# Down stage: two operands read a step earlier, weights a product later

## The chip, the cores and the metric

The kernel runs on one core of a Trainium2 chip. The metric is the device time of one execution in microseconds; the lower the better. One launch computes the whole block, and all arithmetic is done on the core. The core has five engines that run side by side, each with its own instruction order: PE multiplies matrices, ACT applies functions and scaled copies, DVE and POOL work elementwise, and SP issues the DMAs in this program.

## The reference

The block has an attention part and a feed-forward part, each with a residual and a layer norm. The change lies in the last product of the feed-forward part.

```python
x = _layernorm(x + _L0_attn_ref(x, Wq, Wk, Wv, Wo))
x = _layernorm(x + _L0_ffn_ref(x, ...))

def _L0_ffn_ref(input, SU_ug, SU_dp, Wscale_ug, Wscale_dp, W_up, W_gate, W_down):
    x = fwht(x * SU_ug) / SCALE                  # 4096 tokens x 512
    x_up = x @ W_up.T * (Wscale_ug[:INTER] * SCALE)
    x_gate = x @ W_gate.T * (Wscale_ug[INTER:] * SCALE)
    x = jax.nn.silu(x_gate) * x_up               # 4096 x 2048
    x = fwht(x * SU_dp) / SCALE
    x = x @ W_down.T * (Wscale_dp * SCALE)       # 4096 x 512
```

`fwht` is a Walsh-Hadamard transform. The kernel moves the second one into the weights: it transforms W_down once, so that the down product works on silu(gate) times up directly.

## The kernel before

**Arithmetic.** Every fp32 operand is split into a high and a low half[...]: ACT copies the value with rounding into `hi` (line 95), then DVE or POOL subtracts it from the original into `lo` (line 96). `hilo` does both. Each product then takes three matmuls: high by high, high by low, low by high.

**Gate and up.** The loop over `n` (32 steps) computes blocks of gate and up by a scheme of seven half-size products in place of eight. Step n = 31 is the last. Its results and the sums S1 to S4 of them (made by POOL at line 1117, in `hS`) are the seven left-hand operands of the down stage, and are stored to DRAM in `hop_d` by the closures in `late_puts`. Results and sums live in 16 buffers (`utile`, pool `g1`).

**Down.** The tokens are cut into eight units (`units`), and each unit has seven products, s = 0 to 6; (n, s) is product s of unit n. `order` lists them: first units 0 and 1 in turn, (0,0), (1,0), (0,1), (1,1) and so on, then the other units. A product is 48 matmuls of 128x256 at line 1196, into the PSUM tiles `ps_da`, `ps_dc` and `ps_db`. Its left operand is read from `hop_d` in four pieces of 128x512 (`hraw`, 256 KB each; `h_load`) and split by `h_split` into `hah` and `hal`. For s = 0 the operands of units 0 and 1 have tiles of their own, `hxh` and `hxl`. The weights of product s are read from `wdop_d[s]` in four pieces as well (`braw`; `load_b`), split by `split_b` into `wdh`, `wdl`, `wdzh` and `wdzl`, and stay for all units. In this text the first weights are those of s = 0, the second those of s = 1, and so on. Their reads and splits lie between the products of units 0 and 1. DVE adds each finished product to the residual `yres` (line 1206).

**Memory.** All pieces read in this stage, `hraw` as well as `braw` (and before them the weights of gate and up), share one pool of ten buffers:

```python
    rp = ctx.enter_context(tc.tile_pool(name="rp", bufs=10, reuse_waits="tile"))
```

A read is issued when the piece that had its buffer has been split. The split operands `hah` and `hal` have 19 buffers in the pool `d1`, which lies where the pool `g1` of gate and up lay; such a tile can be written when the result or sum that had its place is out of use, and for a sum that is when its store has landed.

**Order.** The kernel's text sets what depends on what and a priority. A scheduler with a time model of its own then puts each engine's instructions into one fixed order. An engine works its list strictly in that order: if an instruction waits, all behind it on that engine wait as well. That holds for SP's queue of DMAs, too.

Of the kernel before, what the change touches and what calls it, by code (L numbers as in the profile page):

```python
# [43 lines left out]
def kernel(  # L44
# [6 lines left out]
    V, S, G, T = nc.vector, nc.scalar, nc.gpsimd, nc.tensor  # L51
# [895 lines left out]
    def h_load(n, s):  # L947
        f, jp = units[n]
        HR[n, s] = []
        for qd in range(4):  # L950
            raw = rp.tile([128, 2, 256], F32, tag="ar", name="hraw")
            dma(raw, hop_d[f][s, jp, :, 2 * qd:2 * qd + 2])
            HR[n, s].append(raw)

    def load_b(s):
        RAW["b", s] = []
        for j in range(4):
            x = rp.tile([128, 2, 256], F32, tag="ar", name="braw")
            dma(x, wdop_d[s][:, 2 * j:2 * j + 2])
            RAW["b", s].append(x)  # L960
# [33 lines left out]
    with ExitStack() as es:  # L994
        pa = es.enter_context(tc.tile_pool(name="g1", bufs=1, reuse_waits="tile"))

        def utile(name):
            return pa.tile([128, 512], F32, tag="u", name=name, bufs=16)

        def araw(name):  # L1000
            return rp.tile([128, 2, 2, 128], F32, tag="ar", name=name)

        def ff_front(i):
            y2 = []
            for e in range(2):
                y = praw.tile([128, 512], F32, tag="raw", name="y_nat")
                dma(y, y_d[2 * i + e])
                y2.append(y)
            yield
            yield from front(i, y2, pa, lambda s, n: pgu.tile(s, F32, tag="a", name=n, bufs=4),  # L1010
                             lambda s, n: pgu.tile(s, F32, tag="a", name=n, bufs=4), (ytile, xtile))

        for s in range(7):
            aload(1, s, araw("A"))
        NS = 32
        yraw, late_puts = [], []
        fr = None
        for n in range(NS):
            f, p = divmod(n, 8)
            bank, sv, c = {}, {}, {}  # L1020

            def emit(u, q, x):
                if u == 1:
                    S.activation(x, x, AF.Silu)  # L1024
                    c["g", q] = x
                else:
                    G.tensor_tensor(x, x, c.pop(("g", q)), ALU.mult)  # L1027
                    c["h", q] = x

            if n in (1, 3, 5, 8):  # L1030
                step(fr, 12)
                fr = ff_front(12 + (1, 3, 5, 8).index(n))
            new = {}
            for s, tag in enumerate(SEQ):
                first = SEQ.index(tag) == s
                wh, wl = AOP.pop((n, s))
                yh, yl = YOPS[s]
                for u in (1, 0):
                    if first:
                        bank[tag, u] = pgu.tile([128, 512], F32, tag=tag, name="ps_" + tag, bufs=4 if tag == "a" else 2)  # L1040
                    ps = bank[tag, u]
                    i = 0
                    for k in range(2):
                        for w, y in ((wh, yh), (wh, yl), (wl, yh)):
                            T.matmul(ps, w[:, u, k], y[:, k], start=first and i == 0, stop=i == 5,  # L1045
                                     skip_group_check=not first)
                            i += 1
                    it = 2 * p + (s >= 4 and s < 6)
                    sc = wsc[:, u, it:it + 1]
                    if s in (0, 2, 4):  # L1050
                        x = pa.tile([128, 512], F32, tag="sv", name="sv", bufs=6)
                        S.activation(x, ps, AF.Copy, scale=sc)  # L1052
                        sv[s, u] = x
                    if s in (1, 4, 6):
                        src, k, q = {1: (ps, 0, 0), 4: (bank.get(("b", u)), 4, 3), 6: (ps, 2, 1)}[s]
                        x = utile("cc")
                        V.scalar_tensor_tensor(x, src, sc, sv[k, u], ALU.mult, ALU.add)
                        emit(u, q, x)
                    if s == 5:
                        if u == 1:  # L1060
                            x = utile("sg")
                            S.activation(x, ps, AF.Silu, scale=sc)
                            c["g", 2] = x
                        else:
                            x = c.pop(("g", 2))
                            V.scalar_tensor_tensor(x, ps, sc, x, ALU.mult, ALU.mult)  # L1066
                            c["h", 2] = x
                if n and s in (1, 2, 3):
                    for _ in range(3):
                        if late_puts:  # L1070
                            late_puts.pop(0)()
                if n + 1 < NS:
                    asplit(n + 1, s)
                if n + 2 < NS:
                    aload(n + 2, s, araw("A"))
                if p == 7:
                    if f < 3:
                        new[s] = ysplit(s, yraw[s])
                        if s < 5:
                            yraw.append(yload(f + 1, s + 2))  # L1080
                    elif s == 0:
                        hx = [praw.tile([128, 2, 256], F32R, tag="raw", name="hxh") for _ in range(3)]
                        hx.append(wres.tile([128, 2, 256], F32R, tag="w", name="hxh"))
                        hy = [ytile([128, 4, 256], F32R, x) for x in ("hxl", "hxl", "hxh", "hxh", "hxl", "hxl")]
                        h_split_x(0, hx, halves(hy[0:2]))
                        h_load(1, 0)
                        y_load(0, 0)
                        y_load(1, 0)
                    elif s == 2:
                        split_b(0)  # L1090
                        load_b(1)
                    elif s == 3:
                        h_split_x(1, halves(hy[2:4]), halves(hy[4:6]))
                        load_b(2)
                    elif s == 4:
                        split_b(1)
                        h_load(0, 1)
                elif n == NS - 2:
                    if s == 4:
                        h_load(0, 0)  # L1100
                    elif s == 6:
                        load_b(0)
                step(fr)
            if p == 6 and f < 3:
                yraw = [yload(f + 1, 0), yload(f + 1, 1)]
            YOPS.update(new)
            H = {"A11": c["h", 0], "A12": c["h", 2], "A21": c["h", 1], "A22": c["h", 3]}

            def put(key, f=f, p=p, H=H):
                dma(hop_d[f][WKEY.index(key)].rearrange("j p i t -> p j i t")[:, :, p],  # L1110
                    H[key].rearrange("p (j t) -> p j t", j=2))

            late_puts = [lambda k=k, put=put: put(k) for k in ("A11", "A12", "A22", "S1", "S3", "S2", "S4")]
            for key, x0, x1, op in (("S1", "A21", "A22", ALU.add), ("S3", "A11", "A21", ALU.subtract),
                                    ("S2", "S3", "A22", ALU.subtract), ("S4", "A12", "S2", ALU.add)):
                H[key] = utile("h" + key)
                G.tensor_tensor(H[key], H[x0], H[x1], op)  # L1117

    with ExitStack() as es:
        pd = es.enter_context(tc.tile_pool(name="d1", bufs=2, reuse_waits="tile"))  # L1120
        order = [(n, s) for s in range(7) for n in range(2)]
# [4 lines left out]
        def h_split(n, s):  # L1126
            HOP[n, s] = []
            for qd, raw in enumerate(HR.pop((n, s))):
                hi, lo = (pd.tile([128, 2, 256], F32R, tag="ad", name=x, bufs=19) for x in ("hah", "hal"))
                hilo(hi, lo, raw, G if qd == 1 or (qd == 3 and s % 2) else V)  # L1130
                HOP[n, s].append((hi, lo))

        def finish(n, half):
# [22 lines left out]

        todo = None
        for idx, (n, s) in enumerate(order):
            if 0 < idx and idx + 1 < len(order):
                h_split(*order[idx + 1])  # L1160
            if n == 0 and s + 2 < 7:
                split_b(s + 2)
            if 0 < idx and idx + 2 < len(order):
                h_load(*order[idx + 2])
            if n == 1 and s + 3 < 7:
                load_b(s + 3)
            for put in late_puts[:3]:
                put()
            late_puts = late_puts[3:]
            if s == 1 and n < 2:  # L1170
                y_load(n, 1, pd)
            if s == 6 and n == 1:
# [18 lines left out]
            for ip, j in ([(ip, j) for j in range(2) for ip in range(8)] if last else  # L1191
                          [(ip, j) for ip in range(8) for j in range(2)]):
                qd, r = divmod(ip, 2)
# [89 lines left out]
```

## Time and profile before

| what | value |
|---|---|
| median of three runs | 2299.53 us (2297.73 to 2301.41) |
| profiled execution | 2299.27 us |
| its span | 2297.6 us, granted clock 0.994 |
| PE busy | 2258.7 us, 98% of the span |
| DVE, ACT, POOL busy | 1757.2, 1393.8, 1280.1 us |
| first matmul of the down stage | 1950.4 us |
| last matmul of gate and up | 1965.1 us |

The profile tells one execution on one core. Its own time is 1.67 us longer than its span, which runs from the first to the last instruction. Durations and places below are microseconds from the span's start. A busy share is an average over the whole kernel; what a change in one stage is worth is read from the waits in that stage. The granted clock is the share of full speed that TensorE was given: 1.00 or, after some pauses, 0.50.

### The profile page before, as it was taken

Reading aid. Unit: us, or ns where it says so; the run is one execution under the profiler, and the core shown is the slowest. Engines: PE = TensorE matmul, PEld = TensorE weight load, DVE = VectorE, ACT = ScalarE, POOL = GpSimd, SP = SyncE. Lnnn points to the kernel's source line nnn. Section 1 sums busy time; section 2 is a strip of 40 time slices with the busy share of each in tenths; the row PEclk is TensorE's granted clock in tenths of the full one; section 3 lists DMA queues with packets and bytes.
Section 4 is the critical chain, followed back from the end, with each engine's and each line's share of the span. In section 5 each row is a group of like instructions: output and inputs, shape, how many; then the busy total and the mean of one; then the engine's idle time right before and its main releaser. Section 6 shows DMA issues by size and latency. Waiting matters only on the chain. (4 is left out here: it accounts for less than half of the span.)

```text
span 2297.6 us, 42221 instructions
## 1 busy us (share of the span) xinstructions
PE 2258.7 (98%) x14432; PEld 2004.3 (87%) x14432; DVE 1757.2 (76%) x2684; ACT 1393.8 (61%) x2515; POOL 1280.1 (56%) x1063
## 2 busy tenths in 40 slices
PE   8999999999999999899999999999999999999998
PEld 7999999899999998688878878878788888899998
DVE  8888888888888878688898775766766766675555
ACT  7777777777777767444443466665555655464553
POOL 5556666555555545568797535665555555633332
PEclk9999999999999999999999999999999999999999
DMA  6665665555555544889998976876765757887773
GB/s 195 176 181 167 184 181 171 168 156 150 167 165 154 170 135 142 301 271 277 284 285 258 309 252 214 253 239 190 230 208 186 242 185 211 260 276 238 227 251 121
DMA packets 369527, 484.15 MB, mean 211 GB/s; under 512 B 68670, under 2 KB 224384, under 8 KB 365344
## 3 DMA queue, kind: packets, MB, share of 16 engines
q1 hardware_dynamic: 369312, 481.45, 68.4%
q8 instruction: 114, 1.87, 0.3%
q14 instruction: 101, 0.83, 0.1%
HBM read 282.76 MB, written 156.76 MB: 191 GB/s over the span
## 5 line engine op out<-in xcount | busy, mean ns | idle before, releaser
L288 PE MATMUL ps_qk<-xh,wh 128*128 128x256 f32 x1280 | 355.3, 278 | 0.0
L288 PE MATMUL ps_qk<-xl,wh 128*128 128x256 f32 x1280 | 354.9, 277 | 0.0
L288 PE MATMUL ps_qk<-xh,wl 128*128 128x256 f32 x1280 | 354.4, 277 | 0.0
L394 POOL TENSOR_SCALAR_AFFINE_SELECT A<-A 64x512 fp32r<-64x512 f32 x256 | 211.5, 826 | 241.8 <-DVE am L390 145.0
L1027 POOL TENSOR_TENSOR cc<-cc 128x512 f32<-128x512 f32 x96 | 149.0, 1554 | 288.8 <-ACT cc L1024 109.7
L96 DVE TENSOR_TENSOR wol<-A,woh 128x512 fp32r<-128x512 f32 x217 | 223.3, 1036 | 104.4 <-ACT woh L95 92.7
L270 POOL TENSOR_TENSOR sw<-sw,csb 128x512 f32<-128x512 f32 x160 | 208.5, 1303 | 135.2 <-ACT sw L269 124.2
L288 PEld LDWEIGHTS ps_qk<-xh,wh 128*128 128x128 f32 x1280 | 240.7, 188 | 3.0
L288 PEld LDWEIGHTS ps_qk<-xh,wl 128*128 128x128 f32 x1280 | 240.4, 188 | 0.9
L288 PEld LDWEIGHTS ps_qk<-xl,wh 128*128 128x128 f32 x1280 | 240.6, 188 | 0.3
L95 ACT ACTIVATE woh<-A 128x512 fp32r<-128x512 f32 x217 | 135.5, 630 | 134.6 <-PE ps_b L1045 76.5
L95 ACT ACTIVATE hah<-hraw 128x512 fp32r<-128x512 f32 x216 | 133.7, 629 | 125.5 <-PE ps_da L1196 63.8
L96 POOL TENSOR_TENSOR hal<-hraw,hah 128x512 fp32r<-128x512 f32 x78 | 106.9, 1374 | 175.2 <-PE ps_da L1196 75.0
L1045 PE MATMUL ps_a<-yoh,woh 128*128 128x512 f32 x512 | 202.6, 397 | 1.2 <-ACT sv L1052 1.0
L1045 PE MATMUL ps_a<-yol,woh 128*128 128x512 f32 x512 | 202.4, 395 | 0.0
L1045 PE MATMUL ps_a<-yoh,wol 128*128 128x512 f32 x512 | 199.8, 396 | 0.0
L96 DVE TENSOR_TENSOR hal<-hraw,hah 128x512 fp32r<-128x512 f32 x138 | 108.7, 796 | 98.0 <-PE ps_da L1196 40.0
L1052 ACT ACTIVATE sv<-ps_a,wsc 128x512 f32<-128x512 f32 x192 | 127.0, 680 | 38.1 <-PE ps_a L1045 37.8
L173 PE MATMUL ps_wo<-wh,oh 128*128 128x512 f32 x372 | 147.8, 397 | 2.1 <-ACT oh L95 2.1
L173 PE MATMUL ps_wo<-wh,ol 128*128 128x512 f32 x372 | 147.6, 397 | 0.0
L173 PE MATMUL ps_wo<-wl,oh 128*128 128x512 f32 x372 | 147.3, 396 | 0.0
L271 DVE TENSOR_TENSOR ps_qk<-ps_qk,csb 128x512 f32<-128x512 f32 x160 | 111.2, 695 | 32.6 <-ACT sw L269 30.9
(280 smaller groups left out, 7356.4 us busy)
## 6 DMA issues: line engine op xcount, KB each, us to landing
hraw<-hop_d SPq DMA_DIRECT2D x224, 256.0 KB
vd<-vhl SPq DMA_DIRECT2D x128, 256.0 KB
num_d<-num SPq DMA_DIRECT2D x128, 256.0 KB
rb<-rec_d SPq DMA_DIRECT2D x128, 256.0 KB
hop_d<-hS SPq DMA_DIRECT2D x128, 256.0 KB
nt<-num_d SPq DMA_DIRECT2D x31, 1024.0 KB
A<-in_wug_dram SPq DMA_DIRECT2D x93, 256.0 KB
hop_d<-cc SPq DMA_DIRECT2D x64, 256.0 KB
```

Of the source, the lines that this page charges most:

```text
L95: i = S.activation(hi, src, AF.Copy)
L96: j = eng.tensor_tensor(lo, src, hi.bitcast(F32), ALU.subtract)
L173: T.matmul(ps, l[:, h], r, start=i == 0, stop=i == 47)
L270: G.tensor_tensor(sw, sw, sinb, ALU.mult)
L271: V.tensor_tensor(ps, ps, cosb, ALU.mult)
L288: T.matmul(ps[:, j], W[key][wa][:, k * 128:(k + 1) * 128], B[xa][:, k], start=i == 0, stop=i == 11)
L394: G.affine_select(ah, ah.bitcast(F32), pattern=[[0, 8], [1, 64]], compare_op=ALU.is_ge, fill=0.0, base=0, channel_multiplier=-1)
L1027: G.tensor_tensor(x, x, c.pop(("g", q)), ALU.mult)
L1045: T.matmul(ps, w[:, u, k], y[:, k], start=first and i == 0, stop=i == 5, skip_group_check=not first)
L1052: S.activation(x, ps, AF.Copy, scale=sc)
```

## The change

In the last step of gate and up (n = 31), the kernel read the third weights, `load_b(2)`, after its step 3 and the operand of (0,1) after its step 4. Now it reads the operand of (0,1) after step 3 and that of (1,1) after step 4. In the down stage the operands of (0,1) and (1,1) are split at the head of the first two products, ahead of the splits of weights there; the third weights are read in the first product and split in the second, and the weights that follow are read in the product of unit 0 before the one of unit 1 that splits them. The subtractions of the operand of (0,1) all go to DVE; before, two of the four went to POOL. The stores of the last step's results and sums are put out in the products 0, 2 and 3 of `order`, where it was 0, 1 and 2.

```diff
                     elif s == 3:
                         h_split_x(1, halves(hy[2:4]), halves(hy[4:6]))
-                        load_b(2)
+                        h_load(0, 1)
                     elif s == 4:
                         split_b(1)
-                        h_load(0, 1)
+                        h_load(1, 1)
...
-                hilo(hi, lo, raw, G if qd == 1 or (qd == 3 and s % 2) else V)
+                hilo(hi, lo, raw, G if (n, s) != (0, 1) and (qd == 1 or (qd == 3 and s % 2)) else V)
                 HOP[n, s].append((hi, lo))
...
         for idx, (n, s) in enumerate(order):
-            if 0 < idx and idx + 1 < len(order):
+            if idx == 0:
+                h_split(*order[2])
+            elif idx == 1:
+                h_split(*order[3])
+            elif 2 < idx and idx + 1 < len(order):
                 h_split(*order[idx + 1])
             if n == 0 and s + 2 < 7:
+                load_b(s + 2)
+            if n == 1 and s + 2 < 7:
                 split_b(s + 2)
-            if 0 < idx and idx + 2 < len(order):
+            if 1 < idx and idx + 2 < len(order):
                 h_load(*order[idx + 2])
-            if n == 1 and s + 3 < 7:
-                load_b(s + 3)
-            for put in late_puts[:3]:
-                put()
-            late_puts = late_puts[3:]
+            if idx in (0, 2, 3):
+                for put in late_puts[:3]:
+                    put()
+                late_puts = late_puts[3:]
```

## The prediction

> **What bounds the kernel now.** I read the page first, then the waits of PE over the last third of the span, then the chain of waits around the one long wait, then the stretches with their clock, and last the timelines of ACT and SP in the same microseconds.
>
> ```profile
> PE 2258.7 (98%) x14432; PEld 2004.3 (87%) x14432; DVE 1757.2 (76%) x2684; ACT 1393.8 (61%) x2515; POOL 1280.1 (56%) x1063
> ```
>
> PE is the bound: 98% of the span. All other work costs time only where PE waits. In the stretch from 1750 us on, the waits of PE hold one entry of size:
>
> ```profile
> PE ps_dc L1196 <- DVE hal L96: 5.4, 1, 5.4
> PE ps_da L1196 <- DVE yres L1206: 1.2, 2, 0.9
> ```
>
> This is product (0,1), the third of the down stage. Its first two matmuls run at 1972.92 and 1973.04; the third needs the low half `hal` of the first quarter and starts at 1978.76. The chain of waits over that place:
>
> ```profile
> 1961.54 4.24 DMA braw<-wdop_d
> ...
> 1967.86 3.88 DMA hop_d<-sg
> 1971.74 1.29 POOL wdzl L96
> 1973.03 2.46 POOL hS L1117 x2
> ...
> 1975.50 2.19 DMA hop_d<-hS
> ...
> 1977.91 0.81 DVE hal L96
> ```
>
> The operand itself has long been there. Its `hal` goes into memory that the sum hS3 of the last gate/up step still holds; that sum is made by POOL behind `wdzl`, the low half of the fourth weights, and is free when its store has landed. (The row "hop_d<-sg" only ended at the same moment: POOL waited for ACT's `wdzh`, and that for its read, as the ACT row at 1971.02 below shows.) The wait also costs clock:
>
> ```profile
> 1972.30:1975.75 3.45, 1.02 (x9) 0.81 (x7) 0.69 (x1) 0.92 (x2) 3.37 (x4) 1.00 0.53 143
> 1975.75:1979.17 3.42, 0.41 (x2) 0.41 (x3) 1.26 (x2) 1.61 (x3) 3.34 (x3) 0.50 0.58 205
> 1979.17:1982.58 3.41, 3.41 (x18) 3.41 (x18) 3.41 (x3) 2.25 (x5) 3.41 (x3) 0.50 0.95 291
> 1982.58:1986.00 3.42, 3.42 (x30) 3.42 (x30) 2.90 (x2) 0.00 (x0) 3.42 (x3) 1.00 0.99 291
> ```
>
> The third figure from the end is the granted clock: half speed from 1975.75 to 1982.58, in two stretches of 3.4 us. PE worked 1978.76 to 1982.58 at half speed, a loss of 3.82/2 = 1.9 us. So wait and clock are worth 5.4 + 1.9 = 7.3 us, 0.32%, and nothing else in this stage is worth 1 us. How long the reads of the down weights take, from SP's issue to ACT's first use:
>
> ```profile
> 1959.14 0.33 SPq L58 DMA_DIRECT2D braw<-wdop_d  x1
> 1961.54 0.32 SPq L58 DMA_DIRECT2D braw<-wdop_d  x1
> 1965.54 0.32 SPq L58 DMA_DIRECT2D braw<-wdop_d  x1
> 1967.19 0.32 SPq L58 DMA_DIRECT2D braw<-wdop_d  x1
> ```
>
> ```profile
> 1964.15 0.63 ACT L95 ACTIVATE wdh<-braw 128x512 fp32r<-128x512 f32 x1 [2.91 <-DMA braw<-wdop_d]
> 1965.81 0.64 ACT L95 ACTIVATE wdh<-braw 128x512 fp32r<-128x512 f32 x1 [1.02 <-DMA braw<-wdop_d]
> 1968.82 0.63 ACT L95 ACTIVATE wdzh<-braw 128x512 fp32r<-128x512 f32 x1 [1.85 <-DMA braw<-wdop_d]
> 1971.02 0.63 ACT L95 ACTIVATE wdzh<-braw 128x512 fp32r<-128x512 f32 x1 [1.57 <-DMA braw<-wdop_d]
> ```
>
> Pair by pair: 5.0, 4.3, 3.3 and 3.8 us. These four numbers carry the forecast.
>
> **The change part by part.** Times are on the clock of the profiled execution before (span 2297.6, own time 2299.27; the median of three runs is 0.26 above that).
>
> *No work is added.* PE's matmuls, the splits and the DMAs are the same in number. The built program's order differs only from 1937 us (third weights) to about 1990. There PE has the same row but for three matmuls moved by 12 places; the fifth to seventh weights stand at the same places of SP's queue, and from 1978.76 on PE ran with a 0.9 us wait at most, each product covering 5.7 us. So "read a product later" costs nothing for those, as long as the products before cover it.
>
> *What goes.* POOL's order is now sums first, then `wdzl` of the fourth weights. POOL reaches cc (before: 1968.62) at about the same time: its new predecessor, `wdzl` of the third weights, ends near 1968.5. Then hS1, hS3 take 2.5 us and hS3 is there at 1972.4 instead of 1975.5: 3.1 us saved on the old chain, 1.3 of them the moved `wdzl` (row 1971.74), 1.8 its wait.
>
> *What comes.* Operands (0,1) and (1,1) are now read in the last gate/up step, eight pieces of 256 KB. All reads of the stage share ten buffers (pool `rp`), and those eight stay taken until the operands are split; their splits still wait for the sums' memory. In the built order ACT's `hah` and DVE's `hal` of (0,1) therefore stand behind all splits of the third and fourth weights, whose eight pieces go through the two buffers left. Piece n+2 is issued when piece n is split, so the reads stand in series. Before, only the fourth weights went that way; now the third do too. On SP's queue the store of hS3 stands behind the last of these reads, too.
>
> The chain, with ACT 0.63, DVE 0.69, POOL 1.3 and 0.03 for each hand-over. Second piece of the third weights: SP issues it at 1957.33, where before a piece of (1,1) went, since both wait for the same POOL subtraction (ends 1957.30); the trace has that transfer landing 3.8 later, 1961.15. ACT starts it at 1961.5 behind a Silu (itself behind the first piece), DVE is done at 1962.85. With L for one read's time: fourth piece issued 1962.9; +L, ACT, POOL: second piece of the fourth weights at 1964.9 + L; +L, ACT, DVE: its fourth piece at 1966.3 + 2L; +L, ACT 0.53 to the next start, `hah` 0.63, `hal` 0.81: PE resumes at 1968.4 + 3L. The store of hS3 (issued 0.4 after that last read, 2.2 to 2.7 to land) is there before L is over, so it doesn't decide.
>
> *L* has no row in this arrangement. The nearest are the four above; the two with the fewest transfers beside them gave 3.3 and 3.8, and the new chain has two reads and a store under way at a time. I take 3.6: resume 1968.4 + 10.8 = 1979.2, 0.4 us later than now. Half clock to 1982.58 again: loss 3.4/2 = 1.7 instead of 1.9. Sum: +0.4 - 0.2 = +0.2 us. Bounds: 2.2 (the fastest store) gives 1975.0, 5.0 (slowest row) 1983.4.
>
> Here a rule speaks otherwise. The Trainium skill, "DMA: Bandwidth & Descriptors", section "Anatomy of one DMA", fits a transfer at about 2.0 us plus bytes/436 GB/s (measured for transfers that GpSimd issues): 2.6 us for 256 KB as an estimate. With it PE resumes at 1976.2: 2.6 us gained, and some 0.4 of clock. All four rows lie above it, by 0.7 to 2.4; I go by the rows.
>
> *ACT blocked in gate/up.* ACT's read-out `sv` (before 1958.43) now waits behind the first piece of the third weights (issued 1956.2, landing as before in 1959.85), so it ends near 1961.1. PE needs that bank at 1962.2: cover 1.1 us, no cost; if that read takes over 4.8 us, PE waits for the excess. Silu, cc and POOL's product behind it have 1.7 us.
>
> *DVE takes all four `hal` of (0,1)*, two from POOL. Row: 7.57 us for five beside a busy POOL, 0.69 alone; PE takes 1.43 a quarter at full clock, 2.6 at half. It resumes at half: no cost; at full clock at most 4 x 0.1 = 0.4.
>
> **The rivals.**
>
> *Rival 1, the wait goes (faster).* For it: the old chain is shorter by 3.1 us, and stores land in 2.2. If L is 2.2 to 2.4, PE resumes at 1975.0 to 1975.6, a wait of some 2.3. On the clock, row and rule differ: the skill's "TensorE: Matmul & The Clock Gate", Part 1, asks for an idle window of 3.4 us before the half clock, while the row 1972.30 was followed by it with PE 30% busy. By the rule 1.9 us of clock is saved as well, by the row perhaps not. Together 3.3 + 1.9 = 5.2 us: 2294.3. Against it: no read of weights here took less than 3.3.
>
> *Rival 2, the two-buffer chain is long (slower).* One mechanism: reads in series, with DVE, POOL and SP's stores waiting in order behind each. With L of 5.1, like the first row, PE resumes at 1983.7: +4.9; the window to 1986.0 is then only two thirds busy, and half clock to 1986.0 or 1989.4 costs 1.2 to 2.9 instead of 1.9. Some +5.2: 2304.7. It passes +0.2% from a mean L of about 5. For it: one row had 5.0, and three such reads add up; against: the mean of the four is 4.1, which gives 1980.7, +1.9 and up to 0.7 of clock, still inside 0.2%.
>
> *Rival 3, the words aren't done.* "Split ahead of the weights" holds for the text; in the built order the splits come after them, for want of memory. This is in the sum already; it is why I don't forecast the gain.
>
> **How the numbers follow.** A chain of one length takes the place of another: 0.56, at 2297.6 + 0.2 for the span, 2299.5 for the profiled kind, with the 0.26 of the median 2299.7. Rival 1 gets 0.16, rival 2 0.28, since the four rows lean to longer reads and every one counts three times. 0.2% is 4.6 us, about what a measurement of this kernel can tell from no change (its three runs spread over 3.7). The case itself, with L from 3.0 (resume at 1977.4, but half clock for 5.2 us: -0.7) to 4.5 (1981.9: +3.3), gives 2298.8 to 2302.8; 8 in 10 reaches into both rivals: 2294.3 to 2305.2.
>
> **What would show it.** Right: POOL's hS start near 1970 in place of 1973; ACT's `wdh` and `wdzh` wait for reads with some 3.6 us each; the chain into `ps_dc` runs over "DMA braw" and not over "hop_d<-hS"; the wait of PE at `ps_dc` is 5 to 7 us and the half clock stays. Wrong: a wait under 3 us with full clock (reads near 2.4), a wait over 9 (reads near 5), or a wait of PE in gate/up before 1965 or at a product after (0,1).

## The result and the profile after

The changed kernel takes 2303.4 us, median of 22 runs (2299.86 to 2309.52). In the same session the kernel before took 2299.53 (22 runs, 2297.58 to 2303.31). The ratio is 1.0016 with a 95% interval of 1.001 to 1.0022: slower by 2.3 to 5.1 us. The profiled execution of the changed kernel took 2299.96, near the short end of its runs, so its trace shows how the time goes, but not all of it. Where one execution is set against another below, "on the clock of before" means that step 29 of gate and up starts at the same time in both; it starts 0.80 us earlier in the first execution of the changed kernel.

The busy share and the waits of PE in the last third:

```profile
PE 2259.4 (98%) x14432; PEld 2005.5 (87%) x14432; DVE 1757.2 (76%) x2686; ACT 1394.9 (61%) x2515; POOL 1279.7 (56%) x1061
```

```profile
PE ps_dc L1201 <- ACT hah L95: 5.6, 1, 5.6
PE ps_da L1201 <- DVE yres L1211: 1.3, 2, 0.9
PE ps_dc L1201 <- DVE hal L96: 0.6, 1, 0.6
```

The wait before product (0,1) is still there and a little longer (5.6 + 0.6 us, before 5.4), but it has another name: PE now waits for `hah` first. The chain of waits over that place says why:

```profile
1966.88 1.30 POOL wdzl L96
...
1968.20 3.31 DMA braw<-wdop_d
...
1971.53 0.65 ACT wdh L95
...
1972.20 0.91 DVE wdl L96
...
1973.12 3.54 DMA braw<-wdop_d
...
1977.22 0.62 ACT hah L95
...
1977.92 1.31 DVE hal L96
...
1979.27 12.79 PE ps_dc L1201 x90
```

Before, the chain was one read, POOL's `wdzl`, two sums and a store. Now it is split, read, split, read, split, and no sum and no store is in it. The read that this chain starts behind, of the fourth piece of the third weights, is issued at 1962.81 and split at 1966.17; POOL makes the sums at 1969.50, ahead of the fourth weights:

```profile
1962.81 0.32 SPq L58 DMA_DIRECT2D braw<-wdop_d  x1
1966.17 0.63 ACT L95 ACTIVATE wdzh<-braw 128x512 fp32r<-128x512 f32 x1 [2.07 <-DMA braw<-wdop_d]
1969.50 3.04 POOL L1117 TENSOR_TENSOR hS<-cc 128x512 f32<-128x512 f32 x2
```

ACT's own timeline shows the reads as the idle time ahead of each split of the fourth weights:

```profile
1968.79 0.64 ACT L95 ACTIVATE wdh<-braw 128x512 fp32r<-128x512 f32 x1 [1.47 <-DMA braw<-wdop_d]
1971.53 0.64 ACT L95 ACTIVATE wdh<-braw 128x512 fp32r<-128x512 f32 x1 [2.10 <-DMA braw<-wdop_d]
1973.64 0.63 ACT L95 ACTIVATE wdzh<-braw 128x512 fp32r<-128x512 f32 x1 [1.48 <-DMA braw<-wdop_d]
1976.68 0.63 ACT L95 ACTIVATE wdzh<-braw 128x512 fp32r<-128x512 f32 x1 [2.41 <-DMA braw<-wdop_d]
1977.22 2.17 ACT L95 ACTIVATE hah<-hraw 128x512 fp32r<-128x512 f32 x4
```

The operand of (0,1) landed before 1950 and lay there; its four splits stand at the end of this row. In the stretches with their clock (third figure from the end) the half clock is there as before, again for 6.8 us, as long as two stretches:

```profile
1972.30:1975.75 3.45, 0.00 (x0) 0.00 (x0) 2.09 (x3) 0.63 (x1) 3.29 (x3) 1.00 0.63 168
1975.75:1979.17 3.42, 0.79 (x2) 0.50 (x2) 1.25 (x2) 2.49 (x5) 1.65 (x2) 0.62 0.81 265
1979.17:1982.58 3.41, 3.31 (x15) 3.31 (x16) 3.41 (x5) 2.82 (x6) 2.07 (x2) 0.50 0.66 141
1982.58:1986.00 3.42, 3.42 (x28) 3.42 (x27) 3.42 (x3) 0.63 (x1) 2.57 (x2) 0.88 1.02 376
```

**A ruler for the stage.** Executions of one kernel reach this place at different times: the first matmul of step 29 of gate and up starts between 1900.3 and 1903.4 us in the five profiled executions of the two kernels. From there on PE's order is nearly the same in all, and every matmul is in the traces. So places below are measured from that start, as differences to the first profiled execution before: to the start of product (1,1), that is with all that (0,1) lost, wait and clock; and to the end of the last matmul.

| execution | to (1,1) | lost in (2,3) and (2,4) | step 29 to the end |
|---|---|---|---|
| before, first | 0 | 0 | 388.36 |
| before, second (b_again) | -0.66 | +3.50 | 391.15 |
| changed, first | +1.43 | +0.10 | 389.83 |
| changed, second (a_again) | +0.85 | +1.04 | 390.21 |
| changed, third (a_third) | +2.26 | +3.25 | 394.25 |
| a_w3early | +0.42 | +1.59 | 390.35 |
| a_w3dve | +3.12 | +1.51 | 392.98 |
| b_w3dve | +1.60 | +0.91 | 390.85 |
| a_rp9 | +5.27 | +0.58 | 394.17 |
| a_rp11 | -4.46 | +5.11 | 392.34 |
| a_pinned, a_pinned2 | -5.45, -5.44 | +1.25, +1.26 | 385.77, 386.82 |
| b_pinned | -3.24 | +0.94 | 386.02 |
| a_pinlay | -5.99 | +0.38 | 384.32 |

What a row's two columns leave over up to the end are small waits between. Products (2,3) and (2,4) are a second place, which the prediction did not have; more on it below.

### The profile page after: what moved, and what is told of

Read it like the earlier page. It is cut to its first block, busy times and chain, and to the rows that moved or that the text cites. A ratio compares the mean times of both kernels' runs of the same rounds, so it can differ in the third digit from the quotient of the medians.

```text
span 2298.2 us, 42218 instructions
## 1 busy us (share of the span) xinstructions
PE 2259.4 (98%) x14432; PEld 2005.5 (87%) x14432; DVE 1757.2 (76%) x2686; ACT 1394.9 (61%) x2515; POOL 1279.7 (56%) x1061
## 4 chain that ended last, share of the span: by engine, by line
PE 89%; DMA 4%; DVE 3%; ACT 2%; issue 1%; POOL 1%; SPq 0%; DVEq 0%; POOLq 0%; ACTq 0%
PE ps_qk L288 17%; PE ps_a L1045 15%; PE ps_wo L173 14%; PE ps_b L1045 7%; PE ps_da L1201 7%; PE ps_num L414 6%; PE ps_v L241 4%; PE ps_s L337 4%; PE ps_c L1045 4%; PE ps_db L1201 3%; PE ps_dc L1201 2%; PE ps_sc L380 1%; PE ps_den L415 1%; PE ps_sc L381 1%; DMA hraw<-hop_d 1%
```

## The experiments

Each experiment is the changed kernel (a_) or the kernel before (b_) with one edit (a_pinlay has two). The kernel before was measured beside them: 2300.11, 2300.22 and 2300.11 us in the three sessions (41, 35 and 51 runs). Theory A is the prediction's: the reads of the third and fourth weights, two buffers at a time, stand in series, and the split of (0,1) behind them. Its rivals are given with each run.

**The changed kernel again, and before again.**

> The changed kernel as it is, another profiled execution. Its 22 timed runs lie between 2299.9 and 2309.5 (median 2303.4), and the first profiled one was among the shortest, at 2299.96. Theory A (reads in series): the excess of a longer execution lies in the three reads of the third and fourth weights that stand in series before product (0,1): PE resumes at 1968.4 plus the sum of their three times, within 0.5 us, and nothing else in the gate/up and down stages differs by 1 us. Theory B (another place): the three reads are as in the first profile (3.3 to 3.5 us) and the excess is a wait of PE in gate/up, because ACT's read-out stands behind a weight split, or more half clock.

> The changed kernel as it is, a third profiled execution, for the spread. Theory A: from the start of step 29 of gate and up to the end it takes 1.4 to 2 us longer than the profiled execution before (which took 388.36), like the two other executions; the wait before product (0,1) is 5.3 to 6.5 us; what differs between executions by more lies ahead of step 29, or at product (2,3), where PE waits for the read of y. Theory B: executions with a wait of 8 us or more before product (0,1) exist, and carry the median of 2303.4.

> The kernel before as it is, a second profiled execution, for the spread. If the first profile before is typical: from the start of step 29 to the end 388.4 within 1, wait before (0,1) 5.1 to 6.1 us, wait at (2,3) about 0.5. If it was a lucky one: 389.5 to 391 by the waits before (0,1) and at (2,3).

The second execution took 2301.78 us, with reads of 3.11, 3.40 and 3.19 us in the series, the third 2302.7 with 3.23, 3.24 and 4.45. On the clock of before PE resumed 1.6 and 1.7 us after 1968.4 plus these reads, not within the 0.5 that I expected; why is told further on. The third took 5.9 us longer from step 29 than the first execution before, where I had 1.4 to 2. In the third the last read alone is 0.9 us longer than in the first:

```profile
1966.66 3.24 DMA braw<-wdop_d
...
1971.52 4.45 DMA braw<-wdop_d
...
1978.59 3.57 PE ps_dc L1201 x15
```

None of the three profiled executions shows a wait of 8 us; the longest timed runs (to 2309.5) were not profiled. The mean of the three at (1,1) is +1.5 us; before (two executions, and a_w3early with the same chain) it is -0.1. At (0,1) the change therefore costs 1.6 us. The other part of the spread is at (2,3). The waits of PE in the second execution before (2301.63 us):

```profile
PE ps_dc L1196 <- DVE hal L96: 4.9, 1, 4.9
PE ps_da L1196 <- DVE yres L1206: 3.2, 2, 2.3
```

Of the second line 2.3 us are that place (the other 0.9 comes near the end in every execution): PE waits for DVE's add into y, and in the chain ahead of the add stands a read, of y or of an operand, that took 5 to 7 us. In the first execution before that wait was 0.3 us. Both kernels have it: 0, 3.5 and 1.6 us for the three with the order of before, 0.1, 1.0 and 3.3 for the changed one. So one profile can be lucky by up to 3 us, and both first ones were.

**The third weights early again.**

```diff
                         h_split_x(1, halves(hy[2:4]), halves(hy[4:6]))
+                        load_b(2)
                         h_load(0, 1)
...
-            if n == 0 and s + 2 < 7:
+            if n == 0 and 2 < s + 2 < 7:
                 load_b(s + 2)
```

> The changed kernel, only the third weights are read after step 3 of the last gate/up step again, ahead of both operands. Theory A (the operands' early reads push the third weights into the two buffers left): SP and POOL are back in the order of before, PE resumes near 1978.8 behind the store of hS3, the chain runs over hop_d<-hS and not over the weights: 2299.5, 4 us less than the changed kernel. Theory B (what costs is the other parts: DVE taking all subtractions of (0,1), the stores put out later, the splits' place): no change from 2303.4.

Measured: 2301.45 us (13 runs), ratio to before 1.0002 (0.9994 to 1.0011), and +0.42 at (1,1). The chain is that of before:

```profile
1969.64 1.30 POOL wdzl L96
1970.94 2.46 POOL hS L1118 x2
...
1973.42 2.09 DMA hop_d<-hS
...
1975.72 0.91 DVE hal L96
```

DVE taking all subtractions of (0,1), the later stores and the place of the splits in the text are all still there. So they cost nothing at (0,1) that stands out from the 0.7 us between the two executions before; the loss there goes with the order of the reads. The time is 2 us over the 2299.5 expected, but not apart from before.

**One buffer fewer, one more.**

```diff
-    rp = ctx.enter_context(tc.tile_pool(name="rp", bufs=10, reuse_waits="tile"))
+    rp = ctx.enter_context(tc.tile_pool(name="rp", bufs=9, reuse_waits="tile"))
```

The other run, a_rp11, has 11 there, and 18 in place of 19 buffers for `hah` and `hal`.

> The changed kernel with nine read buffers instead of ten: one is left for the weights while the eight pieces of the operands are held. Theory A: more reads stand in series before product (0,1): PE resumes 1.5 to 3 us later, near 1981 to 1982, 2305 to 2307, with a wait on a read in the chain. Theory B: the buffers don't matter, 2303.4 as the changed kernel.

> The changed kernel with eleven read buffers (and 18 in place of 19 for the split operands, to make room). Theory A: three buffers for the weights, so one read fewer in series and the fourth weights come some 4 us earlier: the wait of PE before product (0,1) falls from 5.6 to 2 to 3 us, 2295 to 2298. Theory B: no change, 2303.4; theory C (the 18th buffer or the shift of memory costs elsewhere): slower than 2303.4 with a wait at a later product.

With nine, the time was 2303.62 us (21 runs; ratio 1.0015, 1.0008 to 1.0021), the same as the changed kernel. Yet in the stage the trace shows +5.27 at (1,1), 3.8 more than the changed kernel's first, and waits of PE to match:

```profile
PE ps_dc L1201 <- ACT hah L95: 9.5, 2, 9.1
```

That execution took 2300.28, one of the shortest of its 21, and reached step 29 at 1897.9 us, earlier than any other profiled one; that lead was already there at the first matmul of gate and up (1320.0, the others 1322.4 to 1327.9). The buffers act at (0,1) as theory A says, and more strongly than I wrote (1.5 to 3 us); the total did not reach the 2305 to 2307 expected, and with one trace I can't say what made up for it in the others of the 21.

With eleven, the place itself went as theory A says: -4.46 at (1,1), a wait of 1.9 us in place of 6.2, and full clock. But 3.4 us were lost again in small waits up to (0,5), and 5.1 at (2,3), with the half clock there; the time was 2301.61 us (13 runs; ratio 1.0006, 0.9998 to 1.0014), not the 2295 to 2298 expected:

```profile
PE ps_da L1201 <- DVE yres L1211: 4.8, 3, 2.7
PE ps_dc L1201 <- DVE hal L96: 1.9, 2, 1.7
PE ps_db L1201 <- POOL hal L96: 1.0, 1, 1.0
```

Whether the 18 buffers for split operands (one fewer) did this, or other reads that now came first, was not told apart.

**POOL relieved of one split.**

```diff
-            hilo(hl[0][:, 2 * j:2 * j + 2], hl[1][:, 2 * j:2 * j + 2], raw[2 + j], G if j else V)
+            hilo(hl[0][:, 2 * j:2 * j + 2], hl[1][:, 2 * j:2 * j + 2], raw[2 + j], G if j and s != 3 else V)
```

> The kernel before, only that DVE and not POOL makes the low half of the fourth piece of the fourth weights (1.3 us of POOL, 0.7 to 1.3 us of DVE). Theory A (before, PE waits for POOL: that subtraction behind a read, then the sums, then the store of hS3): POOL starts the sums near 1970 instead of 1973.0, PE resumes some 2 to 3 us earlier, a wait of 2.5 to 3.5 us, and 2296 to 2298. Theory B (before, PE waits for something else that ends at the same time, ACT's splits or the read itself): no change, 2300.

> The changed kernel with the same edit as b_w3dve. Theory A: in the changed kernel POOL's subtraction stands behind the sums and off the chain, which runs over the reads: the edit is worth nothing, PE resumes at 1968.4 plus the three reads as before it, and the time is that of the changed kernel, 2303.4 within 1.5. Theory B (POOL and the sums still set the start): 2 to 3 us less, as in b_w3dve.

In the kernel before it gave nothing: 2299.97 us (21 runs), ratio 1.0000 (0.9994 to 1.0007). POOL did start the sums earlier, by 3.1 us when measured from step 29. The rest of the chain:

```profile
1971.26 2.88 POOL hS L1117 x2
...
1976.12 3.55 DMA hop_d<-hS
...
1979.70 1.80 DVE hal L96
```

SP in the same microseconds:

```profile
1974.72 0.32 SPq L58 DMA_DIRECT2D hraw<-hop_d  x1
1975.13 1.45 SPq L58 DMA_DIRECT2D hop_d<-hS  x3
```

hS3 was made at 1974.14, but the stores of hS1 and hS3 stood on SP behind a read that waited until 1974.69 for its buffer. The three stores then went out together and took 3.7 to 4.0 us to land, instead of 2.1 to 2.7, and `hal` took 1.80 instead of 0.81. (The chain names the store issued at 1976.12, but that one landed complete only at 1980.1, after `hal` had begun; the one that `hal` had to wait for was the second, hS3, from 1975.57 to 1979.48.) The expectation missed this: "three us earlier on POOL" was worth nothing, since the queue behind POOL was not free. In the changed kernel the edit brought no gain, as theory A has it: 2304.89 us (7 runs; ratio 1.0024, 1.0012 to 1.0035).

**The order of the text kept.** `hilo` has an argument that keeps its two instructions in the order of the text. It is set for the operand of (0,1) and for the third and fourth weights:

```diff
-            hilo(*hl, raw[j])
+            hilo(*hl, raw[j], V, s in (2, 3))
...
-            ..., raw[2 + j], G if j else V)
+            ..., raw[2 + j], G if j else V, s in (2, 3))
...
-                hilo(hi, lo, raw, ... else V)
+                hilo(hi, lo, raw, ... else V, (n, s) == (0, 1))
```

> The changed kernel, with the splits of the operand of (0,1) and of the third and fourth weights kept in the order of the text on ACT, DVE and POOL: operands first, weights after them (the order that the scheduler had turned round). Reads, buffers and memory are as in the changed kernel. Theory A (the wait before product (0,1) is the read chain, because the splits of (0,1) stand behind all splits of the third and fourth weights): the chain leaves this product; what is left is the store of hS3, with POOL's sums early: hS3 ends near 1972.5, its store lands near 1974.7, PE resumes near 1975.5, a wait of 2 to 3 us instead of 5.7, and full or nearly full clock; about 2297 to 2299, unless the third weights are then late at product (0,2). Theory B (the order on the engines is not what holds PE; the operands' memory is): the wait stays above 5 us and the time at 2303.

> The same kernel as a_pinned, measured again. Theory A: PE waits 1 to 2 us before (0,1), no half clock there, from step 29 to the end 384.5 to 387, and the median is 2 to 3 us under the kernel before. If the first figure was chance: within 1 us of the kernel before.

> The kernel before, with the splits of the third weights, of the operand of (0,1) and of the fourth weights kept in the order of the text on ACT, DVE and POOL, nothing else. POOL then has the sums ahead of the fourth weights, SP has the store of hS3 behind one read of the fourth weights only. Theory A1 (the order on the engines alone makes the wait; reading the operands a step earlier is not needed): PE's wait before (0,1) falls to 1 to 3 us as in a_pinned, 2297 to 2298.5. Theory A2 (the early reads are needed as well, because here the split of (0,1) stands behind the third weights or the store behind a read that waits for a buffer): the wait stays above 4 us and 2300.

The changed kernel with this took 2297.56 us (13 runs; ratio to before 0.9995, 0.9987 to 1.0003) and 2297.27 us (22 runs; 0.9990, 0.9984 to 0.9996). At (1,1) it is 5.4 us ahead of before, both times. The wait before (0,1) and the stretches of the second, and ACT's rows of the operand in the first:

```profile
PE ps_dc L1201 <- DVE hal L96: 1.1, 1, 1.1
```

```profile
1970.20:1973.60 3.40, 2.25 (x19) 2.05 (x18) 1.79 (x3) 2.42 (x5) 1.82 (x2) 1.00 0.48 168
1973.60:1977.00 3.40, 3.36 (x26) 2.95 (x25) 3.40 (x3) 1.34 (x3) 2.34 (x2) 1.00 0.94 332
```

```profile
1963.62 0.62 ACT L95 ACTIVATE hah<-hraw 128x512 fp32r<-128x512 f32 x1
1970.46 2.71 ACT L95 ACTIVATE hah<-hraw 128x512 fp32r<-128x512 f32 x5 [3.58 <-POOL hS L1117]
```

The wait is down to 1.1 us and the half clock is gone, with the same reads, buffers and memory as in the changed kernel. Now the last two pieces of the third weights are read only from 1973.7 on (first of the two executions) and land by 1978.6, in time; (0,2) loses 0.7 and 1.2 us in all, waiting for its own operand, whose read comes later too. The kernel before with the same edit took 2297.95 us (13 runs; 0.9991, 0.9983 to 1.0000), with 3.2 us ahead at (1,1) and this wait:

```profile
PE ps_dc L1196 <- DVE hal L96: 2.4, 1, 2.4
```

So the order alone gives most of it; the rest of the change adds 2.2 us at that product and nothing clear in the total.

**Other memory for the operand.** On top of a_pinned:

```diff
         NS = 32
+        utile("u0")
         yraw, late_puts = [], []
```

> a_pinned, and besides one result buffer is requested ahead of all else in the memory of gate and up, so that results and read-outs change places: the operand of (0,1) then lies where read-outs lay, in its first half, and where the sums lay in its second. Theory A (in a_pinned the wait that is left is the store of hS3 into whose place the first low half goes): the first half starts without a wait over 1 us; but the last quarter waits for the store of hS2, which ends later than hS3's, so the gain of up to 1 us may be given back inside the product: 0 to 1 us less than a_pinned. If what is left in a_pinned is DVE's own order (the add of product (1,0) ahead of the low halves), no change.

2295.11 us (21 runs), ratio to before 0.9981 (0.9975 to 0.9988): the fastest version, 5 us under before by the medians and 8 under the changed kernel. The wait before (0,1) stayed at 1.1 us, so in a_pinned the store was not what was left (there hS3's had landed at 1970.97, and the first `hal` began at 1972.12). The chain shows DVE's add of product (1,0), which waits for PE and stands ahead of the low halves:

```profile
1964.89 8.08 PE ps_da L1202 x68
...
1972.99 0.07 DVE yres L1212
...
1973.60 0.74 DVE hal L96 x2
```

The gain beyond a_pinned is larger than expected (2.2 us by the medians), and its place stays open: in the trace no wait at (0,2) and (1,2) is left, where a_pinned lost 0.7 to 1.2 us, but 0.7 us are lost at (0,3) and 0.8 at (1,4) instead, so that up to the first product of unit 2 the loss is 1.6 us, as in the first execution of a_pinned.

## Why the prediction was right, and where not

The time lies in the range (2294.3 to 2305.2), and by the medians inside 0.2% (3.9 us, 0.17%), the case to which most of the chance went, though the interval of the ratio reaches 0.22%. The mechanism is the forecast one: one chain replaced by another of about the same length. The point 2299.7 was 3.7 us low, and a range 10.9 us wide would have held no change as well: that the time lies in it says little of the sum.

*What goes.* Right. POOL starts the sums at 1970.3 on the clock of before instead of 1973.0, and neither sum nor store is in the chain.

*What comes.* Right in kind: three reads in series, then `hah`, `hal`, PE. The sum read "resumes at 1968.4 + 3L". L was 3.34, 3.31 and 3.54 us in the first execution, 3.4 in the mean of nine reads in the three; I took 3.6. So the reads were 0.6 us shorter in sum than assumed, which by luck hid part of the next error. The Trainium skill's fit ("DMA: Bandwidth & Descriptors", section "Anatomy of one DMA"), estimated there at 2.6, lies below all nine reads. The mis-sized term is 1968.4. In the first execution PE resumes at 1979.27, 0.80 later on the clock of before, 1980.07; less 10.19 for the reads that leaves 1969.9 (1970.0 and 1970.1 in the other two). In the first execution the 1.5 us are DVE's subtractions, which I put at 0.69, from rows without an operation of POOL's beside them, and at 0.81, from a row that met only the end of one. Here they ran beside POOL's:

```profile
1960.93 1.30 POOL L1027 TENSOR_TENSOR cc<-cc 128x512 f32<-128x512 f32 x1 [1.92 <-ACT cc L1024]
1961.38 1.40 DVE L96 TENSOR_TENSOR wdl<-braw,wdh 128x512 fp32r<-128x512 f32 x1 [0.58 <-ACT wdh L95]
1972.20 0.90 DVE L96 TENSOR_TENSOR wdl<-braw,wdh 128x512 fp32r<-128x512 f32 x1 [1.44 <-ACT wdh L95]
1977.39 1.28 POOL L96 TENSOR_TENSOR wdzl<-braw,wdzh 128x512 fp32r<-128x512 f32 x1 [1.27 <-ACT wdzh L95]
```

0.7 and 0.2 us here, and 0.5 on the first `hal` (1.31 in the chain, from 1977.92). Each of the three ended 0.55 to 0.56 us after POOL's operation beside it (at 1962.23, at 1972.54 for the sums, at 1978.67). PE resumed 1.31 us later than before, where I had 0.4.

*The clock.* Two stretches at half speed, as said, but not where I had put them. The half clock ended at 1983.4 (0.88 in the row 1982.58 above), 1984.2 on the clock of before and not 1982.58. PE worked 4.1 us at half speed, a loss of 2.05 us, where I had 1.7 and the kernel before lost 1.91. With the 1.31 that makes 1.45; measured were +1.43 at (1,1), where the sum had +0.2.

*ACT blocked, DVE with all four `hal`.* Right: the products (0,0) and (1,0) start within 0.02 us of before.

*Rivals.* Rival 1 (reads near 2.4) and rival 2 (reads near 5) were both wrong on L: of the nine reads eight took 3.1 to 3.6 us, one 4.45. Rival 3, that "split ahead of the weights" isn't done in the built order, was right and is the cause of the wait: with the order kept, 5 to 6 us come back. But I gave want of memory as its reason, and a_pinned speaks against that: in the same memory ACT wrote three quarters of (0,1) at 1963.62 and 1965.72 and the last one at 1970.46, all ahead of the splits of the third weights (1973.07). The changed kernel wrote the first at 1977.22. Why the scheduler turned the splits round stays open.

*What the sum left out.* "Nothing else in this stage is worth 1 us" held for the one execution that I read; at (2,3) others lost up to 3.5. The three traces put 1.6 us of the loss at (0,1), and none at (2,3), where both kernels lose about the same in the mean (1.7 and 1.5). The runs say 2.3 to 5.1. What lies between is not settled: each mean rests on three executions, and (2,3) alone varies by 3.5 us.

## What to carry to other kernels

Reading data early is no gain when its consumer stands in order behind the work that the early read pushed back: look at the built order of each engine and of the DMA queue, count what then goes through the buffers left, and if need be fix the order of the few instructions that decide. Time an operation from a row with the same neighbours. When a stage of a few us is judged inside a run of milliseconds, measure it from a fixed instruction ahead of it and in more than one execution.

## What the runs showed of the hardware

- DVE's 128x512 subtraction took 0.69 us by itself. Where one of POOL's operations was under way when it began, it took up to 1.8 us and ended 0.55 us after POOL's. Where DVE began first or at the same time, POOL was the one delayed: in the two rows below its sum took 1.82 us instead of 1.3 and ended 1.13 after DVE's. The first executions of both kernels hold 67 cases of the first kind and 55 of the second from 1900 us on, with medians of 0.55 and 1.15 us. The Trainium skill ("SBUF — State Buffer", section "SBUF: two separate sides") states that such an operation with two inputs in SBUF and one of GpSimd lock each other out of a shared port; the rows agree, and the sum should have had it.

```profile
1974.30 0.69 DVE L96 TENSOR_TENSOR wdzl<-braw,wdzh 128x512 fp32r<-128x512 f32 x1 [1.21 <-ACT wdzh L95]
1974.30 1.82 POOL L1117 TENSOR_TENSOR hS<-sg,hS 128x512 f32<-128x512 f32 x1
```

- A store of 256 KB took 2.1 to 2.7 us from issue to landing in the four stores of the sums before, which were issued 1.2 to 1.3 us apart. It took 3.7 to 4.0 where three stores and a read were issued within 1.4 us (b_w3dve), and 3.0 to 4.4 in the changed kernel, where reads of weights and operands were issued among the four.
- In the down stage the half clock began after a stretch of 3.41 us in which PE was busy for 0% (changed, 1973.13 to 1976.54), 29% (before, 1972.34 to 1975.75) or 43% (b_again, 2063.33 to 2066.74). It did not begin after the one with 66% (a_pinned2, 1970.20). It lasted 3.41 us in b_again and 6.83 in the first executions of both kernels. These rows give no threshold: in the kernel before, ahead of this stage, it also began after a stretch with 79% (910.79 to 914.21).
